# Placing the routed experts of a decoder layer among attention and autocorrelation, with their tokens in a weight's buffer

## The chip, the cores and the metric

The kernel runs on one core of a Trainium2 chip, in 32-bit floats throughout. The metric is the device time of one execution in microseconds (us), as the median of several runs; lower is better. The engines are called PE (TensorE: matrix products and transposes), DVE (VectorE), ACT (ScalarE), POOL (GpSimd) and SP (SyncE, which issues the DMAs).

## What is computed

A decoder of two layers, each with three sublayers, every one followed by a residual addition and a layer norm. The batch is 8, the sequence 128, the width 512.

```python
x = norm(x + L0_attn(x))        # 32 heads of 16, causal, with biases
x = norm(x + L0_xattn(x, ctx))  # autocorrelation, 8 heads of 64
x = norm(x + L0_ffn(x))         # base product + 28 routed low-rank experts
x = norm(x + L1_attn(x))        # q,k,v clipped to +-8; norm of q and k; ALiBi; causal
x = norm(x + L1_xattn(x, ctx))  # 16 heads, 4 key heads, of 96
x = norm(x + L1_ffn(x))         # 8 low-rank parts, softmax router
```

The sublayers that the change touches, cut down:

```python
# L0_xattn
corr = ifft(fft(q) * conj(fft(k))).real        # along the sequence, each feature
w, idx = top_k(corr, 9); w = softmax(w)        # 9 lags for each feature
out = sum_i w[i] * v[min(idx[i] + pos, 127)]
# L0_ffn
logits = x @ gate_W.T                          # 28 experts
top_vals, top_idx = top_k(logits, 2); probs = softmax(top_vals)
h = (x @ lora_A.T) * (gate * 2)                # 28 x rank 8
out = x @ base_W.T + h @ lora_B
# L1_attn, the q and k
q = layer_norm(clip(x @ Wq.T)) * q_ln_w + q_ln_b
scores = (q @ k.T) * HEAD_DIM ** -0.5 + slopes * rel
```

## The kernel before, in words

**Tiles.** One batch row is one tile of 128 tokens by 512 features. It stays in SBUF (`xs[b]`) from sublayer to sublayer. There are 8 buffers of 128 x 2048 floats for weights (pool `wp`, tag `w`, used by `weight` and `weight4`): a new weight's DMA waits until the buffer's former holder has been read for the last time. PSUM has four single banks (`bank`) and two pairs of banks (`banks`), each handed round in the order of the program. The tile framework derives each engine's queue from the order in which the program calls the operations, with some moves of its own to interleave them, and adds a wait wherever an operation needs another engine's result or a buffer still in use. Each engine then works strictly through its queue.

**Helpers.** `mm_acc` (L84 to L86) is a chain of products into one bank. `transposed` (L123) turns a tile on PE (L129) and copies the bank out on DVE (L137) or ACT (L139). `add_norm` (L100) adds a bank to the old tokens on DVE (L103), takes the moments (`moments`, L88: statistics L91, aggregation L93, a sum L95, all DVE; the power -0.5 on POOL, L97) and normalises on DVE (L107). If it is given `later`, the part after the sum waits for a call of `catch_up`.

**Attention of layer 0** (loop at L497 to L528). Sixteen steps: four pairs of batch rows times four groups of eight heads. `Heads16` makes a step's scores (L164) into the two double banks, adds the mask on DVE and takes the negated maxima (L181), and `exps` (L193) is sixteen exponentials on ACT. A step later `turn` transposes the exponentials (L212), through double banks again, and the step after that `out` (L229, L235) multiplies by the values. So three steps are in flight. Queries and keys of the next step stand in between, and the output projection of a finished pair (`projection`) in the steps after it.

**Autocorrelation of layer 0** (`Correlated`, L365). For each pair of batch rows: `spectra` (L371) multiplies by a DFT table into two double banks, pa and pb, copies pa out on ACT (xa) and multiplies on DVE (L388, L390) and POOL (L389, L391); `correlate` goes back to lags (pc, copied on ACT to co). Then for each row h: `chosen(h)` finds the nine largest lags (a chain of some 24 small DVE operations, a POOL subtraction L424, ACT's exp, DVE L426 to L430, a POOL product L431); `shifted(h)` turns the weights (wT) and multiplies both them (pw, L445) and the values (pvf) by tables, with copies wf on ACT and products vw on DVE (L453, L455) and POOL; `done(h)` is a last product (poc) and `add_norm`. The pieces of the first two pairs stand beside attention steps 7 to 15. After the loop come `turned.out()`, `prev.turn()`, the third pair's `spectra`, `prev.out()`, two projections, `correlate` and `catch_up`.

**Experts of layer 0.** For each batch row b: `T(b)` turns the tokens (xTf); `R(b)` is the product pg for 28 logits and 224 low-rank values (wlora), then the top two on DVE (L575 to L589, with one exp on ACT), which ends in the weighted values hs; `E(b)` turns hs (hT), sums the base product and the low-rank one into pof (six products of 512 columns), and calls `add_norm`.

**The hand-written order** (L687 to L730) after the attention places T, R and E of rows 0 to 7 between the pieces of the third and fourth autocorrelations (`third`, `fourth`), and near its end the start of layer 1's attention: `turned_tokens` (xTa), `normed` (q and k: product, clip, norm, with weight and bias multiplied and added on POOL from `lnv`, L632 and L633), `values`, `turned_both` (turns of q and k: qT copied on DVE, and kbd, L657, k spread over head pairs by a mask). Then the loop of layer 1's attention begins (L801), which takes E(7) into its first step. The scale of q's scores is multiplied into q's weight and bias once, on POOL (L611).

**Loads.** w1q, w1k (layer 1's query and key weights) are loaded before the attention, w1v, w1o and two weights of the cross attention after it, then alibi and lnv.

Of the kernel before, what the change touches and what calls it, by code (L numbers as in the profile page):

```python
# [17 lines left out]
P = 128  # L18
# [25 lines left out]
def decoder(ctx: ExitStack, tc: tile.TileContext, a: dict, out: bass.AP):  # L44
# [12 lines left out]
    def bank(name):  # L57
        return ps1.tile([P, 512], F32, tag="ps1", name=name)
# [11 lines left out]
    def weight4(key):  # L70
        return weight(key).rearrange("p (c o) -> p c o", c=NC)
# [246 lines left out]
    wbase = weight4("F0_base")  # L318
    wlora = weight("F0_lora")
    w1q = weight4("L1_Wq")  # L320
    w1k = weight4("L1_Wk")
    v_bufs = [values_tiles(ap, i) for i in range(4)]
    vs = {}

# [40 lines left out]
    class Correlated:  # L365
# [2 lines left out]
        def __init__(self, p):  # L368
            self.p, self.bs, self.ex, self.ri = p, (2 * p, 2 * p + 1), [None] * 2, [None] * 2

        def spectra(self):  # L371

            ps = {}
            for n, src in (("a", xs), ("b", cts)):
                ps[n] = banks(f"p{n}_{self.p}")
                for i in range(2):
                    for h, b in enumerate(self.bs):
                        nc.tensor.matmul(
                            ps[n][64 * h : 64 * h + 64, i, :],
                            lhsT=dft[:, T_A + 64 * i : T_A + 64 * i + 64], rhs=src[b], start=True, stop=True,  # L380
                        )
# [91 lines left out]
            ]  # L473


    nc.vector.tensor_scalar(bq4, vecs[:, 0, :], SCALE, None, ALU.mult)
    NP = B // 2
    steps = [(p, f) for p in range(NP) for f in range(NC)]
# [67 lines left out]
    fp = layer.enter_context(stage("f0", 2))  # L546
    kp = layer.enter_context(stage("a1k", 1))
    qp = layer.enter_context(stage("a1q", 2))
    NG = E0 + E0 * R0
    HG = E0 * R0 // 2  # L550
    wga = wlora[:, : NC * NG].rearrange("p (c o) -> p c o", c=NC)
    wlb = wlora[:HG, NC * NG : NC * NG + 2 * D].rearrange("p (j o) -> p j o", j=2)

    lgs = [fp.tile([P, E0 + 6], F32, tag=f"lg{i}", name=f"lg_{i}", bufs=1) for i in range(3)]
    twos = [fp.tile([P, 8], F32, tag=f"two{i}", name=f"two_{i}", bufs=1) for i in range(3)]
    for i in range(3):

        nc.gpsimd.memset(lgs[i][:, E0:], BIG)
        nc.gpsimd.memset(twos[i][:, 2:8], BIG)

    fp_tokens = {}

    def turned_for_experts(b):
        fp_tokens[b] = fp.tile([P, NC, P], F32, tag="xT", name=f"xTf0_{b}", bufs=3)
        transposed(xs[b], NC, P, fp_tokens[b], f"xTf0_{b}", "a")

    def routed(b):

        xT = fp_tokens.pop(b)
        pg = bank(f"pg_{b}")  # L570
        mm_acc(pg[:, :NG], [(xT[:, c, :], wga[:, c, :]) for c in range(NC)])
        lg, two = lgs[b % 3], twos[b % 3]
        nc.scalar.copy(lg[:, :E0], pg[:, :E0])
        top = sm.tile([P, 8], F32, tag="topg", name=f"topg_{b}")
        nc.vector.max(top, lg)  # L575
        nc.vector.tensor_copy(two[:, 0:2], top[:, 0:2])
        lr = fp.tile([P, E0 + 6], F32, tag="lr", name=f"lr_{b}")
        nc.vector.match_replace(lr, two, lg, BIG)
        gx = fp.tile([P, E0], F32, tag="gx", name=f"gx_{b}")
        nc.vector.tensor_scalar(gx, lg[:, :E0], top[:, 0:1], None, ALU.subtract)  # L580
        nc.scalar.activation(gx, gx, AF.Exp)
        nc.vector.scalar_tensor_tensor(gx, lr[:, :E0], BIG, gx, ALU.is_equal, ALU.mult)
        su = sm.tile([P, 1], F32, tag="sug", name=f"sug_{b}")
        nc.vector.tensor_reduce(su, gx, AX.X, ALU.add)
        rc = sm.tile([P, 1], F32, tag="rcg", name=f"rcg_{b}")
        nc.vector.reciprocal(rc, su)
        nc.vector.tensor_scalar(gx, gx, rc, 16.0 / R0, ALU.mult, ALU.mult)
        hs = fp.tile([P, E0, R0], F32, tag="hs", name=f"hs_{b}")
        nc.vector.tensor_tensor(  # L589
            hs, pg[:, E0:NG].rearrange("p (e r) -> p e r", e=E0), bc(gx.unsqueeze(2), [P, E0, R0]), ALU.mult  # L590
        )
        return xT, hs

    def expert_sum(b, xT, hs):
        hT = fp.tile([HG, 2, P], F32, tag="hT", name=f"hT_{b}")
        transposed(hs.rearrange("p e r -> p (e r)"), 2, HG, hT, f"hT_{b}", "a")
        po = bank(f"pof0_{b}")
        mm_acc(
            po,
            [(xT[:, c, :], wbase[:, c, :]) for c in range(NC)] + [(hT[:, j, :], wlb[:, j, :]) for j in range(2)],  # L600
        )
        xs[b] = add_norm(xs[b], po, f"f0_{b}")
# [8 lines left out]
    nc.gpsimd.tensor_scalar(lnv[:, 0:2, :], lnv[:, 0:2, :], SCALE, None, ALU.mult)  # L611
# [37 lines left out]

    def turned_both(b, q, k):  # L650
        qT = ap.tile([P, NC, P], F32, tag="qT", name=f"qT1_{b}")
        transposed(q, NC, P, qT, f"qT1_{b}", "v")
        pt = bank(f"pTk1_{b}")
        for c in range(NC):
            nc.tensor.transpose(pt[:, c * P : (c + 1) * P], k[:, c * P : (c + 1) * P], ident)
# [17 lines left out]

        return bias

    routes = {}

    def route(b):
        routes[b] = routed(b)

    def expert(b):
        expert_sum(b, *routes[b])


    T, R, E = turned_for_experts, route, expert
    third, fourth = autos_of[2:]
    T(0)  # L687
    third.chosen(0)
    R(0)
    T(1)  # L690
    R(1)
    third.shifted(0)
    third.chosen(1)
    E(0)
    T(2)
    third.done(0)
    R(2)
    third.shifted(1)
    fourth.spectra()
    E(1)  # L700
    T(3)
    third.done(1)
    fourth.correlate()
    R(3)
    fourth.chosen(0)
    E(2)
    T(4)
    R(4)
    fourth.shifted(0)
    fourth.chosen(1)  # L710
    E(3)
    T(5)
    xT = turned_tokens(0)
    fourth.done(0)
    R(5)
    E(4)
    fourth.shifted(1)
    raw = [normed(i, 0, xT) for i in range(2)]
    E(5)
    T(6)  # L720
    R(6)
    fourth.done(1)
    autos.close()
    ap = layer.enter_context(stage("a1", 2))
    v = values(0, xT)
    xT = turned_tokens(1)
    qk = turned_both(0, *raw)
    E(6)
    T(7)
    R(7)  # L730

# [501 lines left out]
```

## Time and profile before

| | us |
|---|---|
| median of 3 runs | 923.43 (923.0 to 924.23) |
| the profiled execution | 920.14 |
| its span on the core | 918.3 |
| PE busy | 885.4 (96%) |
| DVE busy | 547.0 (60%) |
| ACT busy | 379.6 (41%) |
| POOL busy | 166.3 (18%) |

The mean granted clock of PE was 0.996. The profile holds one execution. A row of its timeline has the start and the length in us, the engine, the line of the kernel, the operation, the output and inputs by the program's names, shapes, and how many instructions; the bracket at its end is the idle time of the engine just before it and the instruction that released it. In it the attention of layer 0 ends near 232 us, the hand-written stretch near 328, and layer 1's attention begins there.

### The profile page before, as it was taken

Reading aid. Unit: us, or ns where it says so; the run is one execution under the profiler, and the core shown is the slowest. Engines: PE = TensorE matmul, PEld = TensorE weight load, DVE = VectorE, ACT = ScalarE, POOL = GpSimd, SP = SyncE. Lnnn points to the kernel's source line nnn. Section 1 sums busy time; section 2 is a strip of 40 time slices with the busy share of each in tenths; the row PEclk is TensorE's granted clock in tenths of the full one; section 3 lists DMA queues with packets and bytes.
Section 4 is the critical chain, followed back from the end, with each engine's and each line's share of the span. In section 5 each row is a group of like instructions: output and inputs, shape, how many; then the busy total and the mean of one; then the engine's idle time right before and its main releaser. Section 6 shows DMA issues by size and latency. Waiting matters only on the chain.

```text
span 918.3 us, 17042 instructions
## 1 busy us (share of the span) xinstructions
PE 885.4 (96%) x6750; PEld 559.4 (61%) x6750; DVE 547.0 (60%) x1294; ACT 379.6 (41%) x1549; POOL 166.3 (18%) x235
## 2 busy tenths in 40 slices
PE   9999999899899999999999999999999999999985
PEld 5766656564445455565556787585758575865552
DVE  3757788886867668888887215433433353355544
ACT  3876564644232136666666022233223322334220
POOL 2401233233432423344330000000000000000001
PEclk9999999999999999999999999999999999999998
DMA  9700000121200020000030200000000000000000
GB/s 329 301 2 24 2 24 2 58 94 60 91 1 23 1 69 25 2 1 2 2 138 25 70 1 1 24 1 1 1 24 1 1 1 1 1 13 0 24 24 35
DMA packets 9298, 34.40 MB, mean 37 GB/s; under 512 B 1154, under 2 KB 1282, under 8 KB 7298
## 3 DMA queue, kind: packets, MB, share of 16 engines
q1 hardware_dynamic: 9218, 33.31, 10.0%
q8 instruction: 53, 0.87, 0.4%
q14 instruction: 27, 0.22, 0.1%
HBM read 31.21 MB, written 2.10 MB: 36 GB/s over the span
## 4 chain that ended last, share of the span: by engine, by line
PE 79%; DVE 10%; ACT 8%; issue 1%; POOL 1%; DMA 0%; POOLq 0%; SPq 0%; ACTq 0%; DVEq 0%
PE pox L86 9%; PE pqx L86 9%; PE pq L86 5%; PE s_x L878 5%; ACT e_a L193 5%; PE pk L86 5%; PE o_x L932 5%; PE pv L86 5%; PE pkx L86 5%; PE pvx L86 4%; PE pof L86 4%; PE pt_a L212 3%; PE pt_x L915 3%; PE s_a L164 2%; PE po L665 2%; PE o_a L229 1%
## 5 line engine op out<-in xcount | busy, mean ns | idle before, releaser
L193 ACT ACTIVATE e_a<-e_a,m_a 128x128 f32<-128x128 f32 (+1 forms) x512 | 184.8, 365 | 113.8 <-DVE m_a L181 113.8
L193 ACT ACTIVATION_READ_ACCUMULATOR e_a<-e_a,m_a 128x1 f32 x512 | 97.3, 190 | 0.0
L900 ACT ACTIVATE e_x<-s_x,m_x 128x256 f32<-128x256 f32 x128 | 59.1, 488 | 79.1 <-DVE m_x L890 79.1
L86 PE MATMUL pqx<-xTx,w_X_q 128*128 128x256 f32 x384 | 84.8, 380 | 0.0
L86 PE MATMUL pox<-w_X_o,oTx 128*128 128x512 f32 x192 | 84.5, 596 | 0.0
L86 PEld LDWEIGHTS pqx<-xTx,w_X_q 128*128 128x128 f32 x384 | 72.5, 190 | 11.9 <-issue 2.4
L889 DVE TENSOR_REDUCE m_x<-s_x 128x4 f32<-128x1024 f32 x32 | 37.6, 1217 | 54.1 <-PE s_x L878 54.1
L86 PEld LDWEIGHTS pox<-w_X_o,oTx 128*128 128x128 f32 x192 | 35.8, 190 | 48.8 <-issue 44.6
L97 POOL TENSOR_TENSOR rs_x<-ve_x,neghalf 128x1 f32<-128x1 f32 x8 | 4.4, 548 | 324.1 <-DVE ve_x L95 324.1
L181 DVE TENSOR_REDUCE m_a<-e_a 128x4 f32<-128x512 f32 (+1 forms) x128 | 62.6, 542 | 0.0
L792 ACT COPY qTx<-pqx 128x512 f32<-128x512 f32 x24 | 14.1, 588 | 105.8 <-PE pqx L86 105.8
L212 PE MATMUL pt_a<-ident,e_a 128*128 128x128 f32 x384 | 48.6, 274 | 4.9 <-DVE e_a L352 3.9
L878 PE MATMUL s_x<-kTx,qTx 32*128 32x256 f32 x768 | 50.3, 384 | 1.4 <-ACT e_x L900 1.4
L212 PEld LDWEIGHTS pt_a<-ident,e_a 128*128 128x128 f32 x384 | 43.5, 141 | 12.8 <-DVE e_a L352 4.9
L103 DVE TENSOR_TENSOR x_x<-pox,x_a 128x512 f32<-128x512 f32 x8 | 5.5, 692 | 70.5 <-PE pox L86 70.5
L923 ACT COPY pT_x<-pt_x 128x512 f32<-128x512 f32 x32 | 18.8, 591 | 67.8 <-PE pt_x L915 67.6
L878 PEld LDWEIGHTS s_x<-kTx,qTx 32*128 32x128 f32 x768 | 39.9, 184 | 11.2 <-issue 6.4
L932 PE MATMUL o_x<-pT_x,vx 128*32 128x512 f32 x384 | 43.6, 594 | 0.0
L921 DVE COPY pT_x<-pt_x 128x512 f32<-128x512 f32 x32 | 22.0, 687 | 32.0 <-PE pt_x L915 31.9
L164 PEld LDWEIGHTS s_a<-kbd,qT 32*64 32x64 f32 x1024 | 20.7, 131 | 28.1 <-issue 8.9
L906 DVE TENSOR_SCALAR e_x<-e_x,rc_x 128x256 f32<-128x256 f32 x128 | 36.5, 348 | 1.1
L164 PE MATMUL s_a<-kbd,qT 32*64 32x256 f32 (+1 forms) x1024 | 33.2, 335 | 1.8 <-DVE pT_a L213 0.8
(209 smaller groups left out, 1707.6 us busy)
## 6 DMA issues: line engine op xcount, KB each, us to landing
w_X_q<-in_X_q SPq DMA_DIRECT2D x3, 1024.0 KB, 5.1
w_X_o<-in_X_o SPq DMA_DIRECT2D x3, 1024.0 KB, 5.0
w_L_Wv<-in_L_Wv SPq DMA_DIRECT2D x2, 1024.0 KB, 6.3
w_L_Wo<-in_L_Wo SPq DMA_DIRECT2D x2, 1024.0 KB, 8.0
x_in<-in_x SPq DMA_DIRECT2D x8, 256.0 KB, 7.9
ct<-in_ctx SPq DMA_DIRECT2D x8, 256.0 KB, 4.4
cT<-in_ctxT SPq DMA_DIRECT2D x4, 512.0 KB, 3.8
out<-x_f SPq DMA_DIRECT2D x8, 256.0 KB, 2.0
```

The lines of the kernel that those rows point to most:

```text
L86: nc.tensor.matmul(ps, lhsT=l, rhs=r, start=(i == 0), stop=(i == n - 1))
L164: nc.tensor.matmul(s[r // 2][64 * u : 64 * u + 64, r % 2, cols], lhsT=qT[rows, 64 - 64 * part : P - 64 * part], rhs=kbd[rows, :, :keys], s ...
L181: self.scored = nc.vector.tensor_reduce(self.m[:, part, rs, :], self.by_heads(part)[:, rs], AX.X, ALU.max, negate=True)
L193: nc.scalar.activation(e[:, r, x, :], e[:, r, x, :], AF.Exp, bias=self.m[:, part, r, x : x + 1], accum_out=self.su[:, part, r, x : x + 1],)
L212: nc.tensor.transpose(pt[:, r, cols], self.e[:, 2 * i + r, cols], ident)
L878: nc.tensor.matmul(sc[g // 2][:, g % 2, u * 256 : (u + 1) * 256], lhsT=qT[rows, (h0 + u) * NS + n, :], rhs=kT[rows, n], start=(n == 0), st ...
L889: nc.vector.tensor_reduce(self.m[:, 4 * i : 4 * i + 4], self.s[i], AX.X, ALU.max, negate=True)
L900: nc.scalar.activation(self.e[:, j, :], self.s[half][:, i, :], AF.Exp, bias=self.m[:, j : j + 1], scale=1.0 / math.sqrt(XD), accum_out=sel ...
L906: nc.vector.tensor_scalar(self.e[:, j, :], self.e[:, j, :], self.rc[:, j : j + 1], None, ALU.mult)
L915: nc.tensor.transpose(pt[:, i * P : (i + 1) * P], self.e[:, 2 * g + u, s * P : (s + 1) * P], ident)
L921: copied = nc.vector.tensor_copy(o, i)
L932: nc.tensor.matmul(po[32 * g : 32 * g + 32, :], lhsT=v[:, s, g * XD + 32 * n : g * XD + 32 * n + 32], rhs=pT[:, s, g].rearrange("p h t -> ...
```

## The change

**A weight's buffer for the experts' tokens.** w1k is no longer loaded before the attention but after it, ahead of w1v. Its buffer is held by a tile `f0` of 128 x 2048. Each half of it (for even and odd rows) holds a row's xTf (512 columns), hs (224) and hT (256). Before, these lay in a pool of their own, opened after the attention. The three logit tiles and their memsets are made at the start.

**Experts in the attention.** T, R and E are defined ahead of the attention loop (their bodies otherwise unchanged). T(0) and R(0) stand in the attention's step 14, E(0), T(1) and R(1) in step 15. E(1) follows step 14's `out`.

**The third autocorrelation.** Its `spectra` is called ahead of step 14's `out`, not after step 15's `turn`, and its two copies xa are on DVE, not ACT. `correlate` moves between the two projections. `catch_up` comes later, after R(2).

**A new order of the rest**, in the diff: E(2) and E(3) earlier, `done` and `shifted` with other neighbours, `values(0)`, E(6), the tokens of row 1 and `done(1)` of the fourth ahead of `turned_both(0)`.

**The scale** is multiplied in the copy of qT on DVE; the POOL operation on lnv goes. The value tiles' memsets (`v_bufs`) are called after R(5).

```diff
-    w1k = weight4("L1_Wk")
...
-        def spectra(self):
+        def spectra(self, copies="a"):
...
-                    nc.scalar.copy(xa[:, 0:2, :], ps[n])
-
-                    nc.scalar.mul(xa[:, 2, :], ps[n][:, 0, :], sign)
+                    (nc.scalar.copy if copies == "a" else nc.vector.tensor_copy)(xa[:, 0:2, :], ps[n])
+
+                    if copies == "a":
+                        nc.scalar.mul(xa[:, 2, :], ps[n][:, 0, :], sign)
+                    else:
+                        nc.vector.tensor_scalar(xa[:, 2, :], ps[n][:, 0, :], sign, None, ALU.mult)
...
+    f0 = wp.tile([P, 2048], F32, tag="w", name="f0")
+
+    def place(b, begin, n):
+        begin += b % 2 * 1024
+        return f0[:, begin : begin + n]
...
+    experts_at = {14: [lambda: T(0), lambda: R(0)], 15: [lambda: E(0), lambda: T(1), lambda: R(1)]}
...
+        for piece in experts_at.get(n, ()):
+            piece()
...
+    third, fourth = autos_of[2:]
+    third.spectra("v")
     turned.out()
+    E(1)
     prev.turn()
-    autos_of[2].spectra()
     prev.out()
-    for j in range(2):
-        projection(B - 2 + j, oTs[NP - 1])
-    autos_of[2].correlate()
-    catch_up()
+    projection(B - 2, oTs[NP - 1])
+    third.correlate()
+    projection(B - 1, oTs[NP - 1])
     attn.close()
 
+    w1k = weight4("L1_Wk")
...
-    nc.gpsimd.tensor_scalar(lnv[:, 0:2, :], lnv[:, 0:2, :], SCALE, None, ALU.mult)
-
-    v_bufs = [values_tiles(qp, i) for i in range(2)]
+    v_bufs = []
...
-        transposed(q, NC, P, qT, f"qT1_{b}", "v")
+        pt = bank(f"pTq1_{b}")
+        for c in range(NC):
+            nc.tensor.transpose(pt[:, c * P : (c + 1) * P], q[:, c * P : (c + 1) * P], ident)
+
+        nc.vector.tensor_scalar(qT.rearrange("p c t -> p (c t)"), pt, SCALE, None, ALU.mult)
```

The written order, before and after, is this; pieces on one line follow each other:

```
before: T0, chosen3(0), R0, T1, R1, shifted3(0), chosen3(1), E0, T2, done3(0), R2, shifted3(1),
        spectra4, E1, T3, done3(1), correlate4, R3, chosen4(0), E2, T4, R4, shifted4(0), chosen4(1),
        E3, T5, turned_tokens(0), done4(0), R5, E4, shifted4(1), normed q and k, E5, T6, R6, done4(1),
        values(0), turned_tokens(1), turned_both(0), E6, T7, R7
after:  T2, chosen3(0), R2, catch_up, T3, R3, E2, shifted3(0), chosen3(1), spectra4, E3, done3(0),
        correlate4, shifted3(1), T4, R4, chosen4(0), turned_tokens(0), done3(1), E4, T5, R5, memsets,
        shifted4(0), chosen4(1), normed q and k, E5, done4(0), T6, R6, shifted4(1), values(0), E6,
        turned_tokens(1), done4(1), turned_both(0), T7, R7
```

More of the change, by code (lines that the diff above doesn't have):

```diff
@@ L473, in pieces @@
             ]
+    f0 = wp.tile([P, 2048], F32, tag="w", name="f0")
+    def place(b, begin, n):
+        begin += b % 2 * 1024
+        return f0[:, begin : begin + n]
+    NG = E0 + E0 * R0
+    HG = E0 * R0 // 2
+    wga = wlora[:, : NC * NG].rearrange("p (c o) -> p c o", c=NC)
+    wlb = wlora[:HG, NC * NG : NC * NG + 2 * D].rearrange("p (j o) -> p j o", j=2)
+    lgs = [glob.tile([P, E0 + 6], F32, tag=f"lg{i}", name=f"lg_{i}", bufs=1) for i in range(3)]
+    twos = [glob.tile([P, 8], F32, tag=f"two{i}", name=f"two_{i}", bufs=1) for i in range(3)]
@@ new lines, in decoder, with turned_for_experts, routed @@
+    for i in range(3):
+        nc.gpsimd.memset(lgs[i][:, E0:], BIG)
+        nc.gpsimd.memset(twos[i][:, 2:8], BIG)
+    fp_tokens = {}
+    def turned_for_experts(b):
+        fp_tokens[b] = place(b, 0, NC * P).rearrange("p (c t) -> p c t", c=NC)
+        transposed(xs[b], NC, P, fp_tokens[b], f"xTf0_{b}", "a")
+    def routed(b):
+        xT = fp_tokens.pop(b)
+        pg = bank(f"pg_{b}")
+        mm_acc(pg[:, :NG], [(xT[:, c, :], wga[:, c, :]) for c in range(NC)])
+        lg, two = lgs[b % 3], twos[b % 3]
+        nc.scalar.copy(lg[:, :E0], pg[:, :E0])
+        top = sm.tile([P, 8], F32, tag="topg", name=f"topg_{b}")
+        nc.vector.max(top, lg)
+        nc.vector.tensor_copy(two[:, 0:2], top[:, 0:2])
+        lr = sm.tile([P, E0 + 6], F32, tag="lr", name=f"lr_{b}", bufs=2)
+        nc.vector.match_replace(lr, two, lg, BIG)
+        gx = sm.tile([P, E0], F32, tag="gx", name=f"gx_{b}", bufs=2)
+        nc.vector.tensor_scalar(gx, lg[:, :E0], top[:, 0:1], None, ALU.subtract)
+        nc.scalar.activation(gx, gx, AF.Exp)
+        nc.vector.scalar_tensor_tensor(gx, lr[:, :E0], BIG, gx, ALU.is_equal, ALU.mult)
+        su = sm.tile([P, 1], F32, tag="sug", name=f"sug_{b}")
+        nc.vector.tensor_reduce(su, gx, AX.X, ALU.add)
+        rc = sm.tile([P, 1], F32, tag="rcg", name=f"rcg_{b}")
+        nc.vector.reciprocal(rc, su)
+        nc.vector.tensor_scalar(gx, gx, rc, 16.0 / R0, ALU.mult, ALU.mult)
+        hs = place(b, NC * P, E0 * R0).rearrange("p (e r) -> p e r", e=E0)
+        nc.vector.tensor_tensor(
+            hs, pg[:, E0:NG].rearrange("p (e r) -> p e r", e=E0), bc(gx.unsqueeze(2), [P, E0, R0]), ALU.mult
+        )
+        return xT, hs
@@ new lines, in expert_sum, with route @@
+    def expert_sum(b, xT, hs):
+        hT = place(b, NC * P + E0 * R0, 2 * P)[:HG].rearrange("p (j t) -> p j t", j=2)
+        transposed(hs.rearrange("p e r -> p (e r)"), 2, HG, hT, f"hT_{b}", "a")
+        po = bank(f"pof0_{b}")
+        mm_acc(
+            po,
+            [(xT[:, c, :], wbase[:, c, :]) for c in range(NC)] + [(hT[:, j, :], wlb[:, j, :]) for j in range(2)],
+        )
+        xs[b] = add_norm(xs[b], po, f"f0_{b}")
+    routes = {}
+    def route(b):
+        routes[b] = routed(b)
@@ L476, in decoder, with expert @@
+    def expert(b):
+        expert_sum(b, *routes[b])
+    T, R, E = turned_for_experts, route, expert
     nc.vector.tensor_scalar(bq4, vecs[:, 0, :], SCALE, None, ALU.mult)
@@ L545, in decoder @@
     layer = ctx.enter_context(ExitStack())
-    fp = layer.enter_context(stage("f0", 2))
     kp = layer.enter_context(stage("a1k", 1))
     qp = layer.enter_context(stage("a1q", 2))
[L549 to L602, printed above, removed]
     alibi = kp.tile([P, 2, 4, 3 * P], F32, tag="alibi", name="alibi")
@@ L674, in alibi_bias @@
         return bias
[L676 to L687, printed above, removed]
-    third.chosen(0)
-    R(0)
-    T(1)
-    R(1)
+    T(2)
+    third.chosen(0)
+    R(2)
+    catch_up()
+    T(3)
+    R(3)
+    E(2)
     third.shifted(0)
     third.chosen(1)
-    E(0)
-    T(2)
+    fourth.spectra()
+    E(3)
     third.done(0)
-    R(2)
+    fourth.correlate()
     third.shifted(1)
[L699 to L706, printed above, removed]
-    T(4)
-    R(4)
+    T(4)
+    R(4)
+    fourth.chosen(0)
+    xT = turned_tokens(0)
+    third.done(1)
+    E(4)
+    T(5)
+    R(5)
+    v_bufs += [values_tiles(qp, i) for i in range(2)]
     fourth.shifted(0)
     fourth.chosen(1)
[L711 to L717, printed above, removed]
     raw = [normed(i, 0, xT) for i in range(2)]
     E(5)
+    fourth.done(0)
     T(6)
     R(6)
+    fourth.shifted(1)
+    v = values(0, xT)
+    E(6)
+    xT = turned_tokens(1)
     fourth.done(1)
@@ L724, in decoder @@
     ap = layer.enter_context(stage("a1", 2))
-    v = values(0, xT)
-    xT = turned_tokens(1)
     qk = turned_both(0, *raw)
-    E(6)
     T(7)
```

## The prediction

> **What bounds the kernel now.** I read the page's busy shares first, then the chain that ended last, then busy time by stretches around the edited code, then TensorE's (PE) timeline there, last the timelines of VectorE (DVE) and GpSimd (POOL), to see who is late.
>
> ```profile
> PE 885.4 (96%) x6750; PEld 559.4 (61%) x6750; DVE 547.0 (60%) x1294; ACT 379.6 (41%) x1549; POOL 166.3 (18%) x235
> PE 79%; DVE 10%; ACT 8%; issue 1%; POOL 1%; DMA 0%; POOLq 0%; SPq 0%; ACTq 0%; DVEq 0%
> ```
>
> PE is the bound, and the change takes no matmul away (the same products, cut into 1107 groups for 1099). So the time can move only by PE's pauses. They are few (start us : end us, length, then busy us of PE, PEld, DVE, ACT, POOL; the granted clock, 1.00 throughout; DMA share):
>
> ```profile
> 202.40:224.80 22.40, 20.52 (x214) 10.00 (x210) 14.57 (x28) 9.57 (x38) 6.00 (x16) 1.00 0.01 1
> 224.80:240.00 15.20, 11.62 (x73) 8.05 (x73) 14.32 (x75) 4.31 (x10) 7.46 (x8) 1.00 0.57 226
> 240.00:268.00 28.00, 27.60 (x116) 14.08 (x115) 19.01 (x44) 7.67 (x15) 10.72 (x11) 1.00 0.00 1
> 287.00:331.00 44.00, 43.23 (x160) 23.02 (x162) 26.30 (x66) 7.04 (x16) 13.61 (x17) 1.00 0.00 0
> 345.00:505.00 160.00, 158.76 (x1713) 95.11 (x1712) 132.12 (x257) 105.86 (x519) 54.22 (x75) 1.00 0.08 26
> ```
>
> From 202 to 331, all that the change reorders, PE loses little outside 224.8:240. After 345 it is busy 158.76 of 160: a microsecond lost before is late to the end. The pauses one by one, the waited-for in brackets:
>
> ```profile
> 207.95 0.30 PE L229 MATMUL o_a<-pT_a,v 128*32 128x64 f32 x4 [0.88 <-DVE ve_a L95]
> 211.08 0.55 PE L212 MATMUL pt_a<-ident,e_a 128*128 128x128 f32 x3 [0.86 <-ACT e_a L193]
> 232.47 1.97 PE L86 MATMUL pg<-w_F_lora,xTf 128*128 128x252 f32 x8 [1.18 <-ACT xTf L139]
> 235.72 0.66 PE L129 MATMUL pt_wT<-ident,ex 128*128 128x128 f32 x4 [1.29 <-POOL ex L431]
> 237.49 1.98 PE L445 MATMUL pw<-wT,dft 128*128 128x512 f32 x4 [1.11 <-ACT wT L139]
> ```
>
> With 0.40, 0.35, 0.61 and 0.68 at 265.8, 275.7, 280.6 and 313.8 the brackets make 7.36. Between starts each is about 0.16 longer than its bracket (9 x 0.16), and 0.31 at 203.0 and 0.25 at 328.2 show in starts alone: **9.4 us**, the most that any order can win here, plus 1.76 at 350. All waits below are so counted, start to start.
>
> **The change part by part.** I walked the changed order on each queue, every instruction at before's duration, PE strictly in order.
>
> *Experts 0 and 1 in the attention's last steps.* T, R, E of one expert are PE 0.44 + 1.70 + 0.22 + 5.15 = 7.5 us; they only change place, and 186:202.4 before them has PE busy 16.40 of 16.40. What comes with them are waits. pg_0 stands inside the last scores, behind its own turned tokens' copy (ACT 0.59): 0.55. pt_a of step 14 needs the double bank that the bias of the last step frees; that stands on DVE behind expert 0's routing, which waits for pg_0: 1.45. pof_0's second part needs hT's copy, on ACT behind the 16 exps of about 0.36: 1.2. pg_1 0.3. Spectra's xa copies move from ACT to DVE, 1.9 us ahead of the two products of 1.22; the bank they read frees late for the last pt_a: 1.7. pg_2 waits for a token copy behind the lags' exp on ACT: 0.55. hs_2 stands on DVE behind the choice of lags (about 10 us, 228:240 before): 1.0. Sum **6.75**, where before has 6.45 in 202:250: the pauses at 232 to 238 are filled, as many come earlier.
>
> *The others between the last autocorrelations.* Before spread E(0) to E(5), 5.15 us each, between routing and its use. Now four of eight are spent by the time fourth.correlate is through, and the rest has less to lay beside its chains. pvf_5 0.35 and pc 0.4; pg_4 behind wf's copies on ACT (1.01 + 0.59): 1.3; hT_4, whose hs stands on DVE behind the choice of lags, vw and a sum: 2.4; pg_5 0.8; xTf_6 needs the norm of the poc_6 just before (add 0.69, statistics 0.7, two short ones, POOL 0.7, norm 0.55: 3.1 us) with 1.72 us of pvf between: 2.0; pg_6 0.8. Sum **8.05**.
>
> *The end of the stretch.* Before:
>
> ```profile
> 321.82 0.69 DVE L137 COPY qT<-pt_qT 128x512 f32<-128x512 f32 x1
> 322.42 1.21 DVE L657 TENSOR_TENSOR kbd<-pTk,masks 128x1024 f32<-128x1024 f32 x1
> 327.63 0.69 DVE L103 TENSOR_TENSOR x_f<-pof,x_c 128x512 f32<-128x512 f32 x1 [3.99 <-PE pof L86]
> 328.35 0.69 DVE L91 BATCH_NORM_STATS2 st_f<-x_f 128x6 f32<-128x512 f32 x1
> 330.18 0.55 DVE L107 TENSOR_SCALAR x_f<-x_f,mv_f,rs_f 128x512 f32<-128x512 f32 x1 [0.73 <-POOL rs_f L97]
> 322.27 3.60 PE L86 MATMUL pof<-w_F_base,xTf 128*128 128x512 f32 x8
> 327.43 0.60 PE L129 MATMUL pt_xTf<-ident,x_c 128*128 128x128 f32 x4
> ```
>
> qT and kbd, the next attention's operands, are made under pof of E(6). The change puts E(6) and done4(1) ahead of turned_both. After pof_6 PE holds one token turn, poc_7 and the turns of q and k: 0.44 + 1.72 + 0.88 = 3.04 us. DVE's order is: x_f_6's add to norm (3.1, with its wait for POOL in the middle), the add of x_c_7 0.69, qT 0.69, statistics 0.72, kbd 1.21: 6.4 less overlap at the hand-over, 6.2. The first scores wait 3.2; behind them on PE stands xTf_7, which waits for x_c_7's norm, now behind kbd: 1.4; then pg_7 0.6; hT_7, its routing between the bias and max of the first scores, 0.85. Sum **6.05**. At 350 k's chain gets an earlier start, 1.76 becomes about 1.1: **-0.6**.
>
> *Scale and memsets.* [...] Before, POOL scales the norm's weights (2.78 us) and clears the value tiles; the change drops the scaling, and SCALE rides in the qT copy (same 0.69, 128x512 out of PSUM). Beside them:
>
> ```profile
> 223.95 1.42 DVE L107 TENSOR_SCALAR x_a<-x_a,mv_a,rs_a 128x512 f32<-128x512 f32 x1 [0.67 <-POOL rs_a L97]
> 227.76 0.55 DVE L107 TENSOR_SCALAR x_a<-x_a,mv_a,rs_a 128x512 f32<-128x512 f32 x1 [0.67 <-POOL rs_a L97]
> 235.61 1.10 DVE L580 TENSOR_SCALAR gx<-lg,topg 128x28 f32<-128x28 f32 x1
> 235.64 2.78 POOL L611 TENSOR_SCALAR lnv<-lnv 128x1024 f32<-128x1024 f32 x1
> ```
>
> The norm took 1.42 beside the memsets for 0.55 without; gx 1.10 beside the scaling for 0.23 elsewhere: 0.87 each. [...] gx began 0.03 ahead of the scaling and DVE went on under it, so I take the rows: -0.87 of DVE at 235, inside a pause that is filled anyway, and the memsets' 0.87 within the choice of lags; zero on PE, bounds -0.9 and +1.9.
>
> *f0 for the fp pool, w1k later.* The halves of f0 make tokens of b+2 wait for E(b), always long done in the new order: zero; bounds 0 and +0.6 (one turn). That w1k lies now in SP's queue ahead of w1v, w1o, X_k, alibi and lnv, 1 MB at the 226 GB/s of 224.8:240 being 4.6 us, is hidden: k is first projected near 300, alibi is read near 337, and everything landed by 240. If the cover were gone, 4.6. X_v and X_q now wait for E(7), hundreds of us before the cross attention reads them: zero.
>
> Sum: 6.75 + 8.05 + 6.05 - 9.4 - 0.6 = **+10.8 us**. The profiled execution was 920.14 us (span 918.3); it would be 931.0 (span 929.1). The median of the runs, 923.43, stands 3.3 above it, so 934.2; I say 934.
>
> **Rivals.** *The middle's waits shrink* (0.20): each wait lets DVE and ACT catch up, so of 8.05 only half comes: +6.8, 930. For it: DVE is busy 26.3 of 44 in the last stretch; against: the waits are chains with POOL and ACT in them, not throughput. *More POOL in the way* (0.14): the small rs of a norm falls behind POOL's own 1.05 to 1.27 us pieces in three more places, about +4: 938. *Faster* (0.09): the filled pauses of 224.8:240 (3.58 in brackets) leave PE so far behind DVE and ACT that the later waits never open. Its place is the pair hT_4 and first scores; it decides when all waits in 202:350 come to under 11.1. With the attention's steps costing 3, the middle 3 and the end 2.5, that is 8.5, -2.6: 921. Against it: in the end's chain the DVE alone has 6.2 us of work after pof_6, and no lead of DVE shortens that. *Nothing to see* (0.05): half of all waits, about 923.
>
> **How the numbers follow.** The likeliest case, 934, has 0.52. The range 927 to 939 takes in the halved middle, the POOL case and the bounds above and leaves out the two cases at or below no change. A measurement of this kernel tells some 0.2% (1.8 us) from nothing. Faster 0.09, within 0.05, slower 0.86.
>
> **What would show it.** In the changed profile: pauses of PE of about 3 and 1.4 us ahead of layer 1's first scores and the last xTf, released by DVE (kbd, x_c's norm); about 2 each ahead of hT of the fifth expert and xTf of the seventh; 1 to 2 us ahead of pt_a in the last two attention steps; no pause left ahead of pg, wT and pw of the third pair together worth 3.6; PE without gaps from 355 on. It is wrong if PE's pauses from 202 to 350 stay near 9 us, or if PE's work itself grows.

## The result, and the profile after

The changed kernel took 936.42 us in the median of 4 runs (934.3 to 938.84), the kernel before 923.21 in the median of 4 (921.47 to 924.23): a ratio of 1.0148, 95% interval 1.0129 to 1.0168. It is 13.2 us slower; the forecast was 10.8. The profiled execution took 936.25 us with a span of 934.3, which is 16.0 above the span of before, 918.3.

The page of the changed kernel, busy time of PE and the chain that ended last:

```profile
PE 894.4 (96%) x6750; PEld 562.3 (60%) x6750; DVE 547.8 (59%) x1296; ACT 377.9 (40%) x1547; POOL 163.1 (17%) x234
PE 75%; DVE 12%; ACT 9%; issue 1%; POOL 1%; DMA 1%; SPq 0%; POOLq 0%; ACTq 0%; DVEq 0%
```

PE has the same 6750 records and 9.0 us more busy time. No matmul was added, so some ran slower. The forecast had nothing of this, and had named it as a sign that it is wrong ("or if PE's work itself grows"). The other 7.0 us of the 16.0 are idle time of PE; the chain has 3% of the span more on DVE and ACT. The same stretches of time as before (length, busy us of PE, PEld, DVE, ACT, POOL, then the granted clock):

```profile
202.40:224.80 22.40, 20.89 (x197) 11.61 (x195) 15.86 (x44) 8.58 (x41) 2.56 (x5) 1.00 0.16 68
224.80:240.00 15.20, 13.91 (x115) 7.83 (x114) 7.38 (x16) 1.60 (x4) 3.27 (x4) 1.00 0.00 1
240.00:268.00 28.00, 26.37 (x87) 12.39 (x87) 21.61 (x90) 8.22 (x16) 9.54 (x13) 1.00 0.31 122
287.00:331.00 44.00, 40.40 (x113) 20.35 (x114) 25.43 (x74) 7.70 (x16) 16.09 (x18) 0.96 0.04 12
345.00:505.00 160.00, 159.15 (x1621) 92.17 (x1619) 133.90 (x268) 101.87 (x503) 57.16 (x77) 1.00 0.12 43
```

In 224.8:240 PE is now busy 13.91 of 15.20 where it was busy 11.62: the pauses there are filled. From 240 on it loses more than before. After 345 it has hardly a gap, as before, so what was lost stays. PE's pauses of 0.2 us and more in the changed kernel from 202 to 350, each with what ended it (`f` is the tile that now holds xTf, hs and hT):

```profile
207.14 0.87 PE L212 MATMUL pt_a<-ident,e_a 128*128 128x128 f32 x6 [0.98 <-DVE e_a L351]
215.03 1.98 PE L86 MATMUL pof<-w_F_lora,f 112*128 112x512 f32 x4 [0.44 <-ACT f L139]
226.51 0.63 PE L212 MATMUL pt_a<-ident,e_a 128*128 128x128 f32 x4 [1.29 <-DVE pr L392]
245.05 1.97 PE L86 MATMUL pg<-w_F_lora,f 128*128 128x252 f32 x8 [0.32 <-ACT f L139]
251.45 0.43 PE L129 MATMUL pt_hT<-ident,f 128*112 128x128 f32 x2 [1.31 <-DVE f L525]
272.68 1.83 PE L402 MATMUL pc<-dft,pr 64*128 64x128 f32 x28 [0.22 <-POOL pr L393]
279.21 1.12 PE L443 MATMUL pvf<-ct,dft 128*128 128x512 f32 x2 [1.48 <-ACT wf L453]
287.19 0.40 PE L129 MATMUL pt_hT<-ident,f 128*112 128x128 f32 x2 [2.15 <-DVE mv_c L93]
293.86 1.97 PE L86 MATMUL pg<-w_F_lora,f 128*128 128x252 f32 x8 [0.68 <-ACT f L139]
315.79 0.63 PE L129 MATMUL pt_xTf<-ident,x_c 128*128 128x128 f32 x4 [2.00 <-DVE x_c L107]
317.15 3.42 PE L86 MATMUL pg<-w_F_lora,f 128*128 128x252 f32 x8 [0.73 <-ACT f L139]
337.78 1.12 PE L164 MATMUL s_a<-kbd,qT 32*64 32x256 f32 x6 [3.09 <-DVE kbd L682]
339.36 1.09 PE L129 MATMUL pt_xTf<-ident,x_c 128*128 128x128 f32 x4 [0.45 <-DVE x_c L107]
```

For the 2.15 ahead of hT of row 4 the trace names `mv_c`, the next short operation on DVE. What hT reads is hs, which ends just ahead of it; it stands on DVE behind the choice of lags, a row's sum and its statistics:

```profile
286.68 0.37 DVE L525 TENSOR_TENSOR f<-pg,gx 128x224 f32<-128x224 f32 x1
```

The largest, 3.09 us, is the one forecast at 3.2. On DVE it reads as forecast, too: the sum and norm of row 6, then the sum of row 7, then qT, and kbd last.

```profile
334.26 0.55 DVE L107 TENSOR_SCALAR x_f<-x_f,mv_f,rs_f 128x512 f32<-128x512 f32 x1 [0.73 <-POOL rs_f L97]
334.72 0.68 DVE L103 TENSOR_TENSOR x_c<-poc,x_a 128x512 f32<-128x512 f32 x1
335.32 0.68 DVE L677 TENSOR_SCALAR qT<-pTq 128x512 f32<-128x512 f32 x1
335.92 0.68 DVE L91 BATCH_NORM_STATS2 st_c<-x_c 128x6 f32<-128x512 f32 x1
336.52 1.21 DVE L682 TENSOR_TENSOR kbd<-pTk,masks 128x1024 f32<-128x1024 f32 x1
```

The new thing is PE's clock. Cut at the moments at which it changes (length, PE busy, granted clock):

```profile
313.00:316.70 3.70, 1.42 (x6) 1.00 0.00 0
316.70:320.10 3.40, 2.95 (x7) 0.50 0.02 5
320.10:337.20 17.10, 14.59 (x48) 1.00 0.00 0
337.20:344.00 6.80, 5.77 (x24) 0.50 0.00 1
344.00:350.00 6.00, 6.00 (x38) 1.00 0.00 0
```

Behind the pause of 2.00 the clock is halved for 3.4 us, behind that of 3.09 for 6.8. In the profile of before it is 1.00 from 7 us to 911.

So the 16.0 us of the two profiles divide like this, by the starts of the same instructions. Each half clock is reckoned at half of PE's busy time in it; that is an estimate, good to some tenths. Layer 1's first scores start at 337.78 for 327.96: 9.82 late. The first half clock makes half of 2.95 us of it, 1.48. The turn of row 7's tokens (0.53 from its start to the next) lies ahead of these scores before and behind them now, so the waits are 9.82 - 1.48 + 0.53 = 8.87.

The turn of row 1's keys starts at 366.05 for 351.76: 14.29 late, 4.47 more, of which half of 5.77, 2.89, is the second half clock, 0.53 that turn, and 1.05 waits. From there on the difference stays at 14.3 until the last products. The span ends 16.0 later: the clock falls 13.4 us ahead of the end where it was 7.2, and the last two products, 0.70 and 0.59 us before, take 1.22 and 1.06. Together: waits 9.9, half clocks within the edited stretch 4.4, half clock at the end 1.7. Counted so, from start to start, a wait is longer than PE's idle time: the half clocks make 6.1 of the 9.0 us by which PE's busy time grew, and most of the other 2.9 lies in the waits.

### The profile page after: what moved, and what is told of

The parts are those of the page before. It is cut to its first block, busy times and chain, and to the rows that moved or that the text cites. A ratio compares the mean times of both kernels' runs of the same rounds, so it can differ in the third digit from the quotient of the medians.

```text
span 934.3 us, 17037 instructions
## 1 busy us (share of the span) xinstructions
PE 894.4 (96%) x6750; PEld 562.3 (60%) x6750; DVE 547.8 (59%) x1296; ACT 377.9 (40%) x1547; POOL 163.1 (17%) x234
## 4 chain that ended last, share of the span: by engine, by line
PE 75%; DVE 12%; ACT 9%; issue 1%; POOL 1%; DMA 1%; SPq 0%; POOLq 0%; ACTq 0%; DVEq 0%
PE pox L86 9%; PE pqx L86 9%; ACT e_a L193 6%; PE s_x L889 5%; PE o_x L943 5%; PE pq L86 5%; PE pkx L86 4%; PE pk L86 4%; PE pof L86 4%; PE pv L86 4%; PE pvx L86 4%; PE pt_x L926 3%; PE pt_a L212 3%; PE po L690 2%; PE s_a L164 2%
## 5 line engine op out<-in xcount | busy, mean ns | idle before, releaser
L164 PE MATMUL s_a<-kbd,qT 32*64 32x256 f32 (+1 forms) x1024 | 36.0, 339 | 4.9 <-DVE kbd L682 3.1
## 6 DMA issues: line engine op xcount, KB each, us to landing
w_L_Wo<-in_L_Wo SPq DMA_DIRECT2D x2, 1024.0 KB, 10.8
```

Source lines behind the costliest of these rows:

```text
L164: nc.tensor.matmul(s[r // 2][64 * u : 64 * u + 64, r % 2, cols], lhsT=qT[rows, 64 - 64 * part : P - 64 * part], rhs=kbd[rows, :, :keys], s ...
```

## The experiments

My theory after this: the loss is two things, the waits forecast and a half clock that follows a long pause. The rivals: the loss sits in the buffers, the copies or the attention's part; or the half clock comes by itself. "Before" stands for the runs of the kernel before on the same chip.

**The end alone, on the kernel before.**

```diff
     T(6)
     R(6)
-    fourth.done(1)
-    autos.close()
-    ap = layer.enter_context(stage("a1", 2))
     v = values(0, xT)
+    E(6)
     xT = turned_tokens(1)
+    fourth.done(1)
+    autos.close()
+    ap = layer.enter_context(stage("a1", 2))
     qk = turned_both(0, *raw)
-    E(6)
     T(7)
```

> The kernel before with one edit: E(6) and the fourth autocorrelation's done(1) stand ahead of turned_both(0), as in the changed kernel; all else as before. Theory (the pauses of the end, and a half clock that follows a long one): first scores wait about 3.1 us for kbd, xTf and pg of row 7 about 1 more, the wait of k at 350 shrinks by about 1, and if most of 3.4 us is idle the granted clock falls to 0.5 for 3.4 to 6.8 us, which costs 1.5 to 2.8: 927 to 930. Rival (the cost sits in the buffers, the copies or the attention's part): 923, within 1.

929.63 us (928.51 to 932.51), ratio 1.0076 (1.0060 to 1.0093). Half of the loss, from two moved calls. The pause and the clock behind it:

```profile
330.95 1.12 PE L164 MATMUL s_a<-kbd,qT 32*64 32x256 f32 x6 [3.08 <-DVE kbd L657]
```

```profile
327.30:330.70 3.40, 0.56 (x6) 1.00 0.00 0
330.70:337.50 6.80, 6.10 (x25) 0.50 0.00 0
```

The same 3.1 us, and the same 6.8 us of half clock, without any expert in the attention. The rival of the buffers is out for this half.

**The end undone, in the changed kernel.**

```diff
     v = values(0, xT)
-    E(6)
     xT = turned_tokens(1)
     fourth.done(1)
     autos.close()
     ap = layer.enter_context(stage("a1", 2))
     qk = turned_both(0, *raw)
+    E(6)
     T(7)
```

> The changed kernel with turned_both(0) back ahead of E(6). Theory: the waits ahead of the first scores (3.1) and of the last xTf go and with them the half clock of 337 to 344 (2.8 of PE work lost); the fourth's poc of row 7 now waits about 2 us for its products on DVE and POOL, since only values(0) lies between: 930 to 933. Rival (the end does not matter): 936.

932.67 us (930.21 to 934.54), ratio 1.0100 (1.0082 to 1.0119): 3.8 less than the changed kernel. The 3.09 is gone, with the half clock at 337; poc of row 7 waits 0.76 for POOL in its place. It is not the whole 6.9 of the first experiment. In this profile the first half clock lasted 6.8 us for 3.4 (mean clock from 300 to 345 us 0.92): by an estimate it makes 1.7 of the 3.1 that are missing, and the new wait 0.9. Whether the other executions had it so isn't on record.

**The clock by itself.** Products that nobody reads, into the two pauses.

```diff
     fourth.done(0)
+    warm(2)
     T(6)
...
     qk = turned_both(0, *raw)
+    warm(3)
     T(7)
...
+    def warm(n):
+        nobody = bank("nobody_w")
+        for _ in range(n):
+            nc.tensor.matmul(nobody, lhsT=ident, rhs=wbase[:, 0, :], start=True, stop=True)
```

> The changed kernel with five products of 128x512 whose result nobody reads: two between the done of row 6 and its turn of tokens, three between the turns of k and the first scores. They add 4.3 us of PE work inside two pauses of 2.0 and 3.1 us and shorten no chain. Theory (a pause that fills most of a stretch of 3.4 us halves the granted clock after it): clock 1.00 from 310 to 345, time less by 3.5 to 4.5: 932. Rival (the half clock comes at its own times, whatever PE does): the same half clock, 936 or up to 1 more.

933.40 us (932.21 to 935.3), ratio 1.0115 (1.0097 to 1.0132): 3.0 us less, with five more products, a little under the 3.5 to 4.5 expected. The stretches cut as above:

```profile
313.00:316.70 3.70, 3.70 (x9) 1.00 0.00 0
316.70:320.10 3.40, 2.48 (x13) 1.00 0.00 0
320.10:337.20 17.10, 16.98 (x54) 1.00 0.00 0
337.20:344.00 6.80, 5.50 (x46) 1.00 0.02 4
```

No chain is shorter here: kbd is still what the first scores wait for, 0.50 us behind the last of the idle products. Only PE's idleness went, and the half clock with it. So here the half clock followed the pauses, and it is worth about 3 us of the median.

**The buffers and the scale alone.** The changed kernel with the order of before (the diff is the written order in "The change", read backwards, and the attention's end as before). The cross attention's value weight is loaded later here, as this order needs it.

> The changed kernel with the order of before, in the attention and after it, and spectra's copies on ACT: what is left of the change is f0 in w1k's buffer, w1k loaded later, the scale in the qT copy and the early memsets (the cross attention's value weight is loaded after E(7) in the first step of layer 1's attention). Theory: the buffers and the scale cost nothing, 922.5 to 924. Rival (loads or the halves of f0 hold something up): over 925, with a wait of PE on a DMA or of a turn's copy on E.

921.50 us (919.14 to 924.24), ratio 0.9985 (0.9976 to 0.9994). f0, the late w1k and the scale cost nothing in this order; the kernel is even about 1.3 faster. PE's pause ahead of pg at 232 is 0.90 for 1.18, and that ahead of pw 0.68 for 1.11. That doesn't show the gain to be POOL's scaling: the profile of the first experiment, which has the scaling, has 0.67 ahead of pw too, and 1.64 ahead of pg. Where the 1.3 comes from stays open.

**Spectra's copies back on ACT.**

```diff
-    third.spectra("v")
+    third.spectra()
```

> The changed kernel with the third spectra's two copies xa back on ACT. Theory: the 1.29 us pause of PE ahead of the last pt_a of the attention, where the double bank waits for DVE's products behind the copies, goes, and nothing else moves by more than 0.5: 935. Rival (ACT then delays its exponentials and the copies of the turned tokens by the 1.6 us of the copies): 936.5 or later, with new pauses behind ACT.

936.28 us (935.07 to 938.02), ratio 1.0148 (1.0132 to 1.0163): no gain in the time. In the profile the 1.29 is gone and everything after it is 0.7 earlier up to xTf of row 6, which starts at 315.07 for 315.79 although this profile has a half clock of 3.4 us at 175 that the changed kernel's has not. Then the half clock behind that pause lasts 6.8 us, not 3.4 (eight products of pg take 3.73 us for 3.42, the turn of wT behind them 1.06 for 0.60), and the first scores start at 338.40 for 337.78. So the 0.7 us saved did not last to the scores; with 4 runs the time doesn't resolve a gain of 1.3. For the time it is inconclusive.

**The attention's part undone.**

```diff
-    experts_at = {14: [lambda: T(0), lambda: R(0)], 15: [lambda: E(0), lambda: T(1), lambda: R(1)]}
+    experts_at = {}
...
+    T(0)
+    third.chosen(0)
+    R(0)
+    T(1)
+    R(1)
+    E(0)
+    E(1)
     T(2)
-    third.chosen(0)
     R(2)
-    catch_up()
```

with the attention's end, spectra and `catch_up` as before.

> The changed kernel without experts 0 and 1 in the attention: the attention's last steps and spectra as before, then T, R and E of rows 0 and 1 around the third's first choice of lags, then the changed order (the cross attention's value weight is loaded after E(7)). Theory: the pauses of 0.98, 0.44 and 1.29 in the attention turn into 0.88 and 0.88, those of 232 to 252 shrink since 15 us of expert products lie beside the choice of lags, and everything from hT of row 4 on is unchanged (2.15, 2.00, 0.73, 3.09 and the half clocks): 932 to 935. Rival (the loss comes from the attention's part): 927 or less.

942.75 us (940.07 to 943.4), ratio 1.0209 (1.0194 to 1.0224). A clear miss: slower by 6, not faster by 2. With the rest as changed, the two experts are better off in the attention than in this place behind it. Two routings in a row, without other work between them, wait for their own chains:

```profile
233.12 1.97 PE L86 MATMUL pg<-w_F_lora,f 128*128 128x252 f32 x8 [1.45 <-ACT f L139]
237.34 0.68 PE L129 MATMUL pt_hT<-ident,f 128*112 128x128 f32 x2 [2.25 <-DVE f L525]
```

PE's pauses from 200 to 350 come to 18.2 us in brackets for 15.1 in the changed kernel, and half clocks up to 355 to 23.9 us (from 176, 237, 292, 323 and 346 on) for 10.2 (mean clock of the execution 0.983 for 0.987). Half of that difference, at most 6.8 us, is more than the 3.1 of the pauses themselves. (Together they are more than the 6.5 by which the spans differ: 6.8 is an upper bound, as PE is not busy throughout, and the drop of the clock at the end is 6.1 us shorter here, which takes some back.) I had not counted the clock in a single term of that expectation.

**The norm of row 6 under cover.**

```diff
-    E(5)
     fourth.done(0)
+    E(5)
     T(6)
```

> The changed kernel with the fourth's done(0) ahead of E(5) and not behind it, so that pof of 5.15 us covers the norm of row 6. Theory: the pause of 2.00 ahead of the turned tokens of row 6 goes, and with it the half clock at 317 to 320 (1.5 of work); the 3.09 ahead of the first scores stays: 932.5 to 934. Rival (the pause was cover for DVE, and the wait comes back ahead of the first scores): 936.

933.43 us (932.84 to 935.2), ratio 1.0116 (1.0103 to 1.0130): 3.0 less, as expected; the 2.00 is 0.91 and there is no half clock at 317, while the 3.08 ahead of the first scores stays.

**Both repairs of the changed order.** The two diffs together.

> The changed kernel with both repairs of its end: turned_both(0) ahead of E(6), and the fourth's done(0) ahead of E(5). Theory (pauses and the half clocks behind them add): the two single repairs gave 3.8 and 3.0 less than the changed kernel, together 6.5 to 7: 929 to 930; no half clock between 300 and 350. Rival (one of the two only hides the other's wait): 932 or more.

927.00 us (925.32 to 928.04), ratio 1.0045 (1.0033 to 1.0058). 9.4 less than the changed kernel, more than the 6.8 of the two single ones. From 300 to 350 the clock is 1.00, where the changed kernel has 0.89 from 300 to 345. The single repairs each left one long pause and its half clock; which share of the extra 2.6 this is, the profile of one execution can't tell. Two moved calls thus carry over two thirds of the 13.2 us. The rest, 4.4, was not taken apart; this profile still has half clocks of 3.4 us at 176 and 289.

**One expert early, not two.** On the buffers-only kernel: T(0) after spectra, R(0) after the last `out`, E(0) ahead of `third.shifted(0)`, each later E one place earlier, turned_both ahead of E(6).

```diff
     third.spectra()
+    T(0)
     prev.out()
+    R(0)
...
-    T(0)
-    third.chosen(0)
-    R(0)
     T(1)
+    third.chosen(0)
     R(1)
+    E(0)
     third.shifted(0)
     third.chosen(1)
-    E(0)
     T(2)
+    E(1)
     third.done(0)
```

> The kernel before with the change's buffers and scale, and only one expert's turn and routing in the attention's end (after spectra and after the last out), E(0) ahead of the third's first shifted, and from there each E one place earlier; the end with turned_both ahead of E(6) as before. Theory: the pauses ahead of pg, wT and pw at 233 to 238 (2.9 together) are filled by the expert's 7.5 us, later ones grow by less than 1.5 since the end keeps its fill: 919.5 to 921 where the same buffers in the old order gave 921.5. Rival (a pause filled comes back later in full, as in the changed kernel): 921.5 to 925.

920.65 us (919.96 to 922.9), ratio 0.9979 (0.9972 to 0.9987). The time is as expected, but its interval overlaps that of the buffers alone, so a gain by this order is not shown. The way is not as expected: in the profile, of the slowest of these executions, the pauses at 233 to 238 are filled, but one of 1.87 comes at 242 ahead of pw, with a half clock behind it (four products of pw in 2.75 us for 1.98, clock 0.97 from 200 to 250). On ACT the exponential of the second choice of lags stands ahead of the copy that pw waits for, and itself waits 4.04 us for POOL:

```profile
242.18 2.75 PE L447 MATMUL pw<-wT,dft 128*128 128x512 f32 x4 [1.87 <-ACT wT L139]
241.02 0.63 ACT L427 ACTIVATE ex<-ex 128x512 f32<-128x512 f32 x1 [4.04 <-POOL ex L426]
241.56 0.57 ACT L139 COPY wT<-pt_wT 128x512 f32<-128x512 f32 x1
```

**The same, mended.**

```diff
-            nc.scalar.activation(ex, ex, AF.Exp)
+            with tc.issue_after(self.weights.ins) if h and self.p > 1 else nullcontext():
+                nc.scalar.activation(ex, ex, AF.Exp)
...
             transposed(self.ex[h].rearrange("p c t -> p (c t)"), NC, P, wT, f"wT_{b}", "a")
+            self.weights = transposed.copied
...
-    fourth.done(1)
-    autos.close()
-    ap = layer.enter_context(stage("a1", 2))
     v = values(0, xT)
+    fourth.done(1)
+    autos.close()
+    ap = layer.enter_context(stage("a1", 2))
     xT = turned_tokens(1)
```

> The kernel with one expert early, with two mends: in the third and fourth autocorrelation the exponential of the second choice of lags is issued behind the copy of the first one's turned weights, and values(0) stands ahead of the fourth's done(1). Theory: the pauses of 1.87 and 1.18 ahead of pw and of 1.38 ahead of the last hT go, and the half clock after the first: 916 to 918. Rival (the waits move to the next product of the same chain): 920 to 921.

918.13 us (917.81 to 920.63), ratio 0.9957 (0.9944 to 0.9971): faster than both kernels, 4.4 us under the runs of before beside it, and just above the 916 to 918 expected. The pauses that are left between 215 and 350:

```profile
247.87 2.35 PE L86 MATMUL poc<-vw,dft 128*128 128x512 f32 x4 [0.52 <-POOL vw L458]
271.30 1.83 PE L402 MATMUL pc<-dft,pr 64*128 64x128 f32 x28 [0.22 <-POOL pr L393]
292.32 2.35 PE L86 MATMUL poc<-vw,dft 128*128 128x512 f32 x4 [0.82 <-POOL vw L458]
311.89 1.97 PE L86 MATMUL pg<-w_F_lora,f 128*128 128x252 f32 x8 [0.67 <-ACT f L139]
349.75 0.66 PE L684 MATMUL pTk<-ident,k 128*128 128x128 f32 x4 [0.85 <-POOL k L658]
```

3.1 us, for 6.6 between the same instructions of before. So with one expert early, these two mends and the end's cover left in place there was a gain to be had. How much of it the early expert makes is not shown: the mends were not tried without it.

**The pauses of the attention filled.** One product in each of two pauses near 111 and 174, of 1.96 and 1.97 us in before, 1.97 and 1.97 in the changed kernel and 1.97 and 1.96 in the mended one.

```diff
             for i in range(2):
+                if i and self.name in ("a0_2_0", "a0_3_0"):
+                    nc.tensor.matmul(bank("nobody_t"), lhsT=ident, rhs=wbase[:, 0, :], start=True, stop=True)
                 pt = banks(f"pt_{self.name}_{i}")
```

> The mended kernel with one product of 128x512 (0.86 us) that nobody reads between the two halves of pt_a in attention steps 9 and 13, where PE pauses 1.97 us for a double bank in every kernel here. Theory (1.9 us or more of idle PE in one stretch of 3.4 us halves the clock of the next): those two pauses shrink to about 1.1, the half clock that some profiles show at 113 or 176 never comes, and the median falls by the share of executions that had it times 1.7 us: 916.5 to 918, the profile with clock 1.00 up to the end. Rival (that half clock has nothing to do with the pause): 918 to 919, half clocks as before.

> The kernel before with the same two products. Theory: its executions between 921 and 925 differ partly by that half clock; with the pauses filled the median is 921 to 922.5 and the slowest under 924. Rival: 922.6, the same spread.

918.06 us (916.46 to 919.76), ratio 0.9958 (0.9943 to 0.9973), and 922.79 us (919.85 to 923.29), ratio 1.0002 (0.9992 to 1.0013). Both profiles have the clock at 1.00 from 8 us to the end's drop (mean clock 0.995 and 0.996), as expected, but neither time moved: before with the two products missed its 921 to 922.5, and its executions still spread over 3.4 us. So the half clock near 113 or 176, as the mended kernel's profile has it behind the first of these pauses (six turns in 1.45 us for 0.87), is not what spreads the times. The spread does go with the clock: of the 78 executions of before beside these experiments the five with a mean granted clock of 0.996, as in its profile, took 920.1 to 920.9 us, and the 27 with 0.992 took 922.7 on average. The end's drop, which came 7.2 us ahead of the last instruction in the profile of before and 13.4 in the changed kernel's, may be part of it; that wasn't tried.

## Why the prediction was right, and where it was short

The time and its direction were right, and so was the mechanism as far as it went: waits come up where fill was taken away. One term was missing, PE's clock, and that the number came out near is in part luck.

**The waits.** The walk gave 10.8, the profile 9.9. Up to the first scores it gave 8.85 (6.75 + 8.05 + 3.2 less 9.15 of before) and 8.87 came; from there on it gave 2.0 and about 1.1 came. By parts, in brackets, to which about 0.16 each is added between starts. (Up to the first scores the listed pauses make 16.6 so, the starts say 18.0. Pauses too short for the list are 0.1 of the rest; the other 1.3 is busy time of PE, in part perhaps half clock that the estimate above has too small. So the close match of 8.85 and 8.87 is no proof of each part.)

- The attention's part, 6.75: too large. The pauses of 0.98, 0.44, 1.29, 0.32 and 1.31 make 4.3, or 5.1 between starts. pt_a and pof were forecast at 1.45 and 1.2, and of the waits of pg_0, pg_1 and pg_2 (1.4 together) only one of 0.32 shows. It was still a step in the right place: 1.29 for the 1.7 ahead of the last pt_a, released by DVE's product as forecast.
- The middle, 8.05: 0.22, 1.48, 2.15, 0.68, 2.00 and 0.73 make 7.3, or 8.2 between starts. hT of row 4 was forecast at 2.4, xTf of row 6 at 2.0.
- The end, 6.05: 3.09 for 3.2 ahead of the first scores. Behind it the walk was too dark: 0.45 for 1.4, and the 0.6 and 0.85 of pg_7 and hT_7 did not come, probably because PE, at half clock, came later to what it would have waited for. The end's own run confirms the chain as the cause.
- Scale and memsets. I went by two rows, and the later rows point both ways. With POOL's scaling gone, the gx that the prediction read takes 0.22 to 0.23 us in all eight rows of the changed kernel. But in the buffers-only kernel, which has no scaling either, a gx that starts 0.1 us behind a subtraction on POOL takes 0.99 for 0.21 and ends with it. And in the profile of the first experiment, where the scaling came later since it waited for its load, a gx in the midst of it takes 0.22. The first two rows are of the buffers-only kernel, the other two of that experiment:

```profile
238.38 1.05 POOL L426 TENSOR_TENSOR ex<-co,top 128x512 f32<-128x512 f32 x1 [1.68 <-DVE rcg L522]
238.47 0.99 DVE L523 TENSOR_SCALAR gx<-gx,rcg 128x28 f32<-128x28 f32 x1
236.76 2.87 POOL L611 TENSOR_SCALAR lnv<-lnv 128x1024 f32<-128x1024 f32 x1 [0.82 <-DMA lnv<-in_L_ln]
237.72 0.22 DVE L587 TENSOR_SCALAR gx<-gx,rcg 128x28 f32<-128x28 f32 x1
```

  So neither 0.87 nor 2.78 is a price of the scaling as such. The gain was taken at zero on PE, with bounds of -0.9 and +1.9. No run shows the +1.9; the buffers-only run gained 1.3 (0.6 to 2.2 by its interval). I can't say how much of it is the scaling.
- f0 and w1k at zero: shown by the same run for the order of before; in the changed kernel none of the listed pauses waits for a load.

**What the sum lacked** is PE's clock. I took every product at before's duration, and before has one clock, 1.00, wherever the change works. The pauses of 2.0 and 3.1 us cost themselves and then half of the work of the next 3.4 and 6.8 us: in the profile 4.4 us in the stretch and 1.7 at the end, in the medians about 3 by the run with idle products. The premise that did not hold is "So the time can move only by PE's pauses".

**Luck.** The forecast lacked 6.1 us of half clock and was 0.9 too long in its waits; the profiles are 16.0 apart. That the medians are only 13.2 apart, within the range, is because before's profile is one of its fast executions (920.14, clock 0.996, for a median of 923.43), while the changed kernel's lies at its median (936.25 for 936.42). By the executions beside the experiments (922.7 at 0.992, 920.3 at 0.996 on average) most of this 3.3 is reduced clock, so the median of before has some of it as well. Had I added the 6.1 in full, 940 would have come out, beyond the range.

The case "more POOL in the way", which pointed to 938, did not happen: in the list of pauses none is put down to a norm's small POOL operation.

**The rivals.** "Faster" hung on the first scores and hT of row 4; both waited as written. "The middle's waits shrink" did not hold either.

## What to carry to other kernels

When work is moved to fill a pause, write down what it covered in its old place: here E(6) covered the making of qT and kbd and E(5) the norm of row 6, and moving two calls gave back more than two thirds of the loss. Leave one piece of fill at each place where a chain has nothing else over it. Here, with PE busy for 96%, a pause of 2.00 us cost itself and by estimate 1.5 us of half clock behind it, one of 3.09 itself and 2.9, and one of 2.15 itself alone; the next section shows where the three lay.

## What the runs showed of the hardware

In the profile of the changed kernel PE's clock is 1.00 for 310.61 us (from 6.09 to 316.70), 0.50 for 3.41, 1.00 for 17.07, 0.50 for 6.83 and 1.00 for 576.85; in that of before it is 1.00 for 904.53 (from 6.57 to 911.11). These are 91, 1, 5, 2, 169 and 265 times 3.413 us. So in both profiles the changes lie on a grid of 3.41 us. I laid it over both and took PE's idle time in each cell between 20 and 900 us. These are the two cells that a half clock followed, the fullest of idle time that none followed, and the two that the pause of 2.15 lies in:

| profile | cell, us | PE idle, us | clock in the next cell |
|---|---|---|---|
| changed | 313.29 to 316.70 | 2.28 | 0.50, for one cell |
| changed | 333.77 to 337.18 | 2.49 | 0.50, for two cells |
| changed | 173.34 to 176.75 | 1.81 | 1.00 |
| before | 108.97 to 112.39 | 1.80 | 1.00 |
| changed | 282.57 to 285.98 | 0.93 | 1.00 |
| changed | 285.98 to 289.39 | 1.21 | 1.00 |

In these two profiles, then, the half clock went with the idle time of one cell: the pause of 2.00 lay within one, that of 2.15 was cut in two by the grid. The half clock that lasted one cell had 0.45 us of idle PE in it, the one that lasted two had 1.05 in the first; two cases make no rule. Nor do these rows tell whether the sum in a cell or its longest piece decides, or how much it takes.

The other runs agree that a pause's length alone does not settle it. In the run with both repairs the pause ahead of hT of row 4 is 2.16, and the eight products behind it take 5.13 us from first start to the next product's, where behind the changed kernel's 2.15 they take 3.43. In the mended kernel six turns behind the pause of 1.97 take 1.45 us, behind that of 1.96 they take 0.87.
